# A convolution block on one core: later weights spread over 27 images, small statistics steps on other engines, a new order of the beginning

## The chip, the cores and the metric

The kernel runs on one core of a Trainium2 chip. The metric is the device time of one execution in microseconds; lower is better. The five engines work through queues of their own: TensorE (PE; its weight loads are PEld), VectorE (DVE), ScalarE (ACT), GpSimd (POOL) and SyncE (SP, which here only issues DMAs). They wait for each other by semaphores. A difference of 0.2%, about 2.5 us, is what a measurement of this kernel can tell from no change.

## The reference

`x` holds 160 images of 128 channels, 32 x 32 in float32. Each image is normalised in groups of four channels, the weights are rounded to two coarse levels that depend on the range of all weights, a 3 x 3 convolution runs with one of five weight sets, and the image itself is added.

```python
beta, alpha = max(U), min(U)                  # over all five sets
s1 = (beta - alpha) / 3;   v1 = s1 * floor(U / s1)
s2 = s1 / 5;               v2 = s2 * floor((U - v1) / s2)
w  = (v1 + v2).reshape(128 * 5, 128, 3, 3)
g  = x in 32 groups of 4 channels             # per image
gn = (g - mean(g)) / sqrt(var(g) + 1e-5)
out = x + conv3x3(gn, w, groups=5)            # image 5 b + n uses set n
```

## The kernel before

**Layout.** Channels lie on the 128 partitions, an image is a row of 1024 float32 numbers in each. The images are ordered by weight set: 32 images of set 0, then 32 of set 1 and so on; loads and stores move four images at a time (`load`, `residual`).

**Weights.** `weight_range` (L352) reduces each of the five raw sets to a maximum and a negated minimum on VectorE; `over_partitions` (L365) takes the maximum over the partitions with two TensorE transposes, a VectorE reduction and a TensorE matmul against `ones`, and `Steps.from_range` (L43) derives the step sizes in 20 VectorE instructions on one number per partition. `make_column` (L384) makes one of the three columns of 3 x 3 kernels: 17 VectorE instructions on 128 x 384 numbers (`quantise`, L95, `floor_div`, L81; the last one, L392, writes `m`), then three TensorE transposes (L398), two ScalarE copies (L400, L401) and three GpSimd sums (L403 to L405). It is a generator: `take(column, k)` issues its next k instructions, so that they can be laid between other work. `qpool` has one buffer of each kind.

**Images.** `measure` (L409) finds mean and variance of an image: even ones by VectorE's `bn_stats` (L152, L153), odd ones by two ScalarE passes, sum (L159) and squares (L168), each followed by a small GpSimd step (L161, L162, L171). `Statistics` then goes over a group of up to eight images: `means` (matmul with the group matrix, L177), `deviations` (four VectorE steps, L185 to L189), `variances` (matmul, L192), `scales` (a VectorE step L197, then on GpSimd the power L199 and three small steps L201, L204, L205). `normalise` (L431) and `high_part` (L439) run on ScalarE, `low_part` (L444) and `combinations` (L458 to L461: `d` and `st`) on VectorE. The image is split in a high and a low half-precision part; `conv` (L497) multiplies `st` into the bank pair `m` first (L505), then the high part into `eo` (L478) with `d` (L505). `leave` (L531) copies `m` to `mm` on ScalarE, `add_pairs` makes the pair sums `pq` on VectorE (L540, L541) and TensorE adds them to `eo` (L544). `residual` (L551) adds the image on VectorE and the store is issued on SP. Images 0 to 2 (`FIRST`) go another way: `conv_direct` (L489) adds the high and the low part, 12 matmuls per column of the weights.

**Order.** The order of all instructions is written out by hand in `run` (L562). First come loads and constants, then the beginning up to the three weight columns of set 0, then a loop over the images. In turn i of the loop come: the group matmuls of statistics that are ready, the convolution of image i, the normalisation of i + 3, sums, `leave(i)`, the high part of i + 3, the low part and the combinations of i + 2, `add_pairs(i)`, `residual(i - 1)`, the small statistics steps, the measuring of image i + 13, and the next steps of the next weight set:

```python
if b == self.per_set * 3 // 8 and n + 1 < N_SETS:
    later = (s for col in self.COLS for s in self.make_column(n + 1, col))
if later is not None:
    take(later, 4)
```

`b` counts the images of a set, 0 to 31, so a set's columns are made from image 12 on, four VectorE instructions per image. Each engine works in the order of issue.

The lines that the change touches: `from_range` (L43), `deviations` (L181), `scales` (L194), `weight_range` and `over_partitions` (L352, L365), `measure` (L409), `residual` (L546) and `run` (L562). The functions:

## Time and profile before

| | us |
|---|---|
| median of 3 executions | 1235.76 |
| lowest, highest | 1235.52, 1237.92 |
| profiled execution | 1238.82 |
| its span | 1237.1 |
| TensorE busy | 1134.9 (92%) |
| VectorE busy | 979.9 (79%) |
| ScalarE busy | 678.1 (55%) |
| GpSimd busy | 234.7 (19%) |

The page splits the span in 40 slices of 31 us. TensorE's busy share is below 90% in the slices 1 to 4 and in some later ones, and its granted clock is below full speed in slices 2 to 4. Busy shares are averages over stages with different limits, so what follows goes by stage: which wait ends last there. In rows, `L398` is the line of the kernel; `out<-in` are the program's names; `[1.07 <-DVE m L392]` is the idle time of the engine just ahead of the instruction and what ended it. VectorE instructions of one row overlap a little, so that the distance from start to start is what one costs.

### The profile page before, as it was taken

The numbers are of one execution on the slowest core, as the hardware profiler recorded it, in microseconds if no ns is written. First come the engines' busy times: TensorE is split into PE (matmuls) and PEld (weight loads), VectorE is DVE, ScalarE is ACT, GpSimd is POOL, SyncE is SP. The second block draws the span as 40 slices with busy tenths as digits, with TensorE's granted clock in tenths as the row PEclk, the third lists the DMA queues.
The fourth block names the chain that finished last, engine by engine and source line by source line (L and its number), as shares of the span: only waits on it lengthen the run. The fifth ranks groups of instructions, "written<-read, shape, count | busy, mean of one in ns | idle before, by whom it ended". The sixth has DMA issues, their size and how long they took to land.

```text
span 1237.1 us, 16052 instructions
## 1 busy us (share of the span) xinstructions
PE 1134.9 (92%) x6215; PEld 612.2 (49%) x6215; DVE 979.9 (79%) x1751; ACT 678.1 (55%) x829; POOL 234.7 (19%) x392
## 2 busy tenths in 40 slices
PE   0378999899999998999999999999999999999997
PEld 0134555445555544555555445555544555555553
DVE  7657889987777999777789997777999877777662
ACT  1444755556665555565655555656555565656440
POOL 2121211212121112212121212121112212121100
PEclk9878999999999999999999999999999999999999
DMA  9103333333334333444433333333333444431113
GB/s 379 56 1 134 139 137 136 136 136 137 136 136 152 132 139 129 163 173 179 162 136 136 136 137 136 136 137 138 135 136 137 176 170 179 156 136 69 69 69 138
DMA packets 43140, 171.82 MB, mean 139 GB/s; under 512 B 1456, under 2 KB 1456, under 8 KB 43056
## 3 DMA queue, kind: packets, MB, share of 16 engines
q1 hardware_dynamic: 42768, 169.55, 36.5%
q8 instruction: 50, 0.82, 0.3%
q10 hardware_dynamic: 288, 1.18, 0.2%
q14 instruction: 34, 0.28, 0.1%
HBM read 86.84 MB, written 83.89 MB: 138 GB/s over the span
## 4 chain that ended last, share of the span: by engine, by line
PE 62%; DVE 31%; POOL 3%; issue 2%; ACT 1%; DMA 0%; DVEq 0%; POOLq 0%
PE eo L478 34%; PE m L505 12%; PE eo L505 11%; DVE xt L551 5%; DVE lo L444 4%; PE eo L544 4%; DVE st L152 3%; DVE d L458 2%; DVE pq L541 1%; POOL rstd L199 1%; DVE tt L91 1%; DVE pq L540 1%; DVE tt L92 1%; DVE st L460 1%; DVE tt L89 1%
## 5 line engine op out<-in xcount | busy, mean ns | idle before, releaser
L478 PE MATMUL eo<-hi,wt 128*128 128x512 f16 (+1 forms) x2862 | 690.9, 378 | 1.1 <-ACT wt L400 1.1
L478 PEld LDWEIGHTS <-wt 128*128 128x128 f16 x2934 | 290.2, 99 | 283.6 <-issue 17.2
L505 PEld LDWEIGHTS <-wt 128*128 128x128 f16 x2826 | 277.7, 99 | 221.5 <-issue 8.9
L531 ACT ACTIVATE mm<-m 128x1024 f16<-128x1024 f32 x157 | 160.3, 1021 | 353.3 <-PE m L505 353.1
L505 PE MATMUL eo<-d,wt 128*128 128x256 f16 (+1 forms) x1884 | 283.3, 273 | 0.0
L431 ACT ACTIVATE z<-xt,shift,rstd 128x1024 f32<-128x1024 f32 x160 | 198.1, 1238 | 99.9 <-POOL shift L205 99.9
L505 PE MATMUL m<-st,wt 128*128 128x512 f16 x942 | 235.2, 387 | 3.2 <-DVE xt L551 3.2
L551 DVE SCALAR_TENSOR_TENSOR xt<-eo,s2z,xt 128x1024 f32<-128x1024 f32 x159 | 202.9, 1276 | 8.4 <-PE eo L478 5.9
L444 DVE TENSOR_TENSOR lo<-z,hi 128x1024 f16<-128x1024 f32 x160 | 193.2, 1207 | 3.8 <-ACT hi L439 3.8
L540 DVE TENSOR_TENSOR pq<-mm 128x512 f16<-128x512 f16 x157 | 66.3, 422 | 144.3 <-ACT mm L531 139.4
L439 ACT CAST hi<-z 128x1024 f16<-128x1024 f32 x160 | 165.9, 1037 | 0.2
L458 DVE TENSOR_TENSOR d<-lo 128x1024 f16<-128x1024 f16 x157 | 109.5, 697 | 58.8 <-PE eo L505 48.2
L161 POOL TENSOR_SCALAR minus<-total 128x1 f32<-128x1 f32 x80 | 19.2, 240 | 462.0 <-ACT junk L159 462.0
L152 DVE BATCH_NORM_STATS2 st<-xt 128x6 f32<-128x512 f32 x160 | 102.0, 679 | 0.0
L544 PE MATMUL eo<-pq,up 128*128 128x512 f16 x314 | 93.5, 379 | 7.6 <-DVE pq L541 7.6
L171 POOL TENSOR_SCALAR mv<-squares 128x1 f32<-128x1 f32 x80 | 52.7, 660 | 231.4 <-ACT junk L168 231.4
L168 ACT ACTIVATE junk<-xt,minus 128x1024 f16<-128x1024 f32 x80 | 91.9, 1149 | 1.8 <-POOL minus L161 1.8
L159 ACT ACTIVATE junk<-xt 128x1024 f16<-128x1024 f32 x80 | 83.5, 1044 | 9.7 <-DMA xt<-in_x_dram 9.7
L199 POOL TENSOR_TENSOR rstd<-ve,mhalf 128x8 f32<-128x8 f32 (+2 forms) x23 | 47.2, 2052 | 167.3 <-DVE ve L197 167.3
L460 DVE TENSOR_TENSOR st<-lo 128x512 f16<-128x512 f16 x157 | 67.5, 430 | 0.0
L461 DVE TENSOR_TENSOR st<-lo 128x512 f16<-128x512 f16 x157 | 66.5, 423 | 0.0
L541 DVE TENSOR_TENSOR pq<-mm 128x512 f16<-128x512 f16 x157 | 65.5, 417 | 0.0
(89 smaller groups left out, 450.9 us busy)
## 6 DMA issues: line engine op xcount, KB each, us to landing
xt<-in_x_dram SPq DMA_DIRECT2D x39, 2048.0 KB, 12.6
out_dram<-xt SPq DMA_DIRECT2D x39, 2048.0 KB, 7.6
xt<-in_x_dram SPq DMA_DIRECT2D x4, 512.0 KB, 9.7
out_dram<-xt SPq DMA_DIRECT2D x4, 512.0 KB, 3.7
u<-in_L_conv_U_dram SPq DMA_DIRECT2D x3, 576.0 KB, 7.6
u<-in_L_conv_U_dram ACTq DMA_DIRECT2D x2, 576.0 KB, 6.6
```

The lines of the kernel that those rows point to most:

```text
L152: self.nc.vector.bn_stats(st[:, h, :], image[:, h * half : (h + 1) * half])
L159: nc.scalar.activation(junk, image, ACTF.Copy, accum_out=total)
L168: nc.scalar.activation(junk, image, ACTF.Square, bias=self.minus[j], accum_out=squares)
L431: nc.scalar.activation(z, self.image(i), ACTF.Identity, bias=st.shift[:, j : j + 1], scale=st.rstd[:, j : j + 1],)
L439: self.nc.scalar.copy(hi.rearrange("p h w -> p (h w)"), self.z[i])
L444: self.nc.vector.tensor_sub(lo[:, 1 : self.H + 1, :].rearrange("p h w -> p (h w)"), self.z.pop(i), self.hi[i].rearrange("p h w -> p (h w)"),)
L458: nc.vector.tensor_sub(d, lo[:, 0:H, :], lo[:, 2 : H + 2, :])
L478: nc.tensor.matmul(target[:, h, r0 - h0 : r1 - h0, c0:c1], self.wts[n, col][:, k, :], tile[:, s0 : s0 + r1 - r0, c0 + dw : c1 + dw], start ...
L505: nc.tensor.matmul(target[:, :, c0:c1], self.wts[n, col][:, kind, :], source[:, :, c0 + dw : c1 + dw], start=start, stop=stop,)
L531: self.nc.scalar.mul(m, self.m.pop(i).rearrange("p a i w -> p a (i w)"), DOWN)
L544: nc.tensor.matmul(to, self.up, pq[:, h], start=False, stop=True)
L551: self.nc.vector.scalar_tensor_tensor(xj, eo.rearrange("p h r w -> p (h r w)"), self.steps.s2z, xj, ALU.mult, ALU.add,)
```

## The change

- **Later weights.** The columns of the next set begin at image 4 of a set, not 12, and two instructions are taken per image, not four: 27 images.
- **Statistics.** `deviations` copies the negated mean with ScalarE (`ngm`) and does its three steps on GpSimd; in `scales` ScalarE copies the variance out of PSUM and one GpSimd step adds EPS and brings the factor in, so that two GpSimd steps behind the power fall away. No VectorE step is left in either.
- **Beginning.** All raw weight sets are loaded on the SP queue, set 0 in two halves, which are also reduced one by one. `from_range` becomes a generator and reads the spread from PSUM; its steps are issued alternately with those of the first column. Images below 8 (`EARLY`) are all measured by ScalarE, pairwise. The order of measuring, statistics, columns and first convolutions is new.
- **Loop.** `residual(i - 1)` is issued ahead of `add_pairs(i)`. The pool of `d` and `st` has four buffers, not three.
- **End.** The last image's residual and store go in two halves.

```diff
     def from_range(self, extg):
...
-        span = col("span")
-        nc.vector.tensor_add(span, extg[:, 0:1], extg[:, 1:2])
-        self.s1 = divide_exact("s1", span, 3.0)
-        self.parts1 = parts("s1", self.s1)
...
+        yield nc.vector.tensor_reduce(span, extg, AX.X, ALU.add)
+        yield from divide_exact("s1", self.s1, span, 3.0)
+        yield from parts(self.parts1, self.s1)
+        yield from divide_exact("s2", self.s2, self.s1, 5.0)
+        yield from parts(self.parts2, self.s2)
...
     def deviations(self):
-        nc.vector.tensor_copy(self.gm, self.pg[:, 0, :])
+        nc.scalar.mul(self.ngm, self.pg[:, 0, :], -1.0)
-        nc.vector.tensor_sub(self.dv, mv[:, :, 0], self.gm)
-        nc.vector.tensor_mul(self.dv, self.dv, self.dv)
-        nc.vector.tensor_add(self.dv, self.dv, mv[:, :, 1])
+        nc.gpsimd.tensor_tensor(self.dv, mv[:, :, 0], self.ngm, ALU.add)
+        nc.gpsimd.tensor_tensor(self.dv, self.dv, self.dv, ALU.mult)
+        nc.gpsimd.tensor_tensor(self.dv, self.dv, mv[:, :, 1], ALU.add)
...
     def scales(self):
-        nc.vector.tensor_scalar_add(ve, self.pg[:, 1, :], EPS)
+        nc.scalar.copy(ve, self.pg[:, 1, :])
+        nc.gpsimd.tensor_scalar(ve, ve, EPS, self.scale**-2, ALU.add, ALU.mult)
         nc.gpsimd.tensor_tensor(self.rstd, ve, self.mhalf[:, : self.nb], ALU.pow)
-        if self.scale != 1.0:
-            nc.gpsimd.tensor_scalar_mul(self.rstd, self.rstd, self.scale)
-        nc.gpsimd.tensor_tensor(self.shift, self.gm, self.rstd, ALU.mult)
-        nc.gpsimd.tensor_scalar_mul(self.shift, self.shift, -1.0)
+        nc.gpsimd.tensor_tensor(self.shift, self.ngm, self.rstd, ALU.mult)
...
-        self.rows = pool("rows", 3)
+        self.rows = pool("rows", 4)
...
     def weight_range(self, us):
+        pieces = [us[0][:, : P // 2], us[0][:, P // 2 :], *us[1:]]
...
     def over_partitions(self, ext1, ident):
...
-        extg = self.const.tile([P, 2], F32, tag="extg", name="extg")
-        nc.vector.tensor_copy(extg, spread)
-        self.steps.from_range(extg)
+        return spread
...
     def measure(self, i, stages=(0, 1)):
-        if i % 2 == 0:
+        if i % 2 == 0 and i >= self.EARLY:
...
     def residual(self, i):
+        halves = [slice(0, 512), slice(512, 1024)] if i == self.imgs - 1 else [slice(0, 1024)]
+        for h in halves:
...
     def run(self):
-            (nc.sync, nc.scalar)[n % 2].dma_start(un, self.uv[n])
+            half = P // 2 if n == 0 else P
+            for c in range(0, P, half):
+                nc.sync.dma_start(un[:, c : c + half], self.uv[n][:, c : c + half])
...
+        spread = self.over_partitions(self.weight_range(self.us), ident)
+        chain = self.steps.from_range(spread)
+        column = self.make_column(0, 1)
+        take(chain, 6)
+        take(column, 1)
+        take(chain, 1)
+        take(column, 1)
+        take(chain, 2)
+        take(column, 1)
+        for _ in range(7):
+            take(chain, 1)
+            take(column, 1)
+        run(chain)
+        measure(0, 1)
+        self.stats[0].means()
         self.stats[0].deviations()
         self.stats[0].variances()
+        measure(2, 3)
         self.stats[0].scales()
+        self.stats[1].means()
         self.normalise(0)
         self.high_part(0)
+        self.stats[1].deviations()
+        self.stats[1].variances()
         self.normalise(1)
         self.high_part(1)
+        self.stats[1].scales()
+        run(column)
         self.low_part(0)
         self.low_part(1)
         self.normalise(2)
         self.high_part(2)
         self.normalise(3)
         self.high_part(3)
+        self.conv_direct(0, 1)
+        self.conv_direct(1, 1)
+        column = self.make_column(0, 0)
+        take(column, 5)
         self.low_part(2)
+        measure(4, 5)
         run(column)
+        measure(6, 7)
         self.conv_direct(2, 1)
+        self.conv_direct(0, 0)
         self.stats[2].means()
         self.stats[2].deviations()
+        self.conv_direct(1, 0)
         self.stats[2].variances()
         self.stats[2].scales()
+        self.conv_direct(2, 0)
+        run(self.make_column(0, 2))
...
-            if i >= self.FIRST:
-                self.add_pairs(i)
             if i < self.FIRST:
                 self.residual(i)
             elif i > self.FIRST:
                 self.residual(i - 1)
+            if i >= self.FIRST:
+                self.add_pairs(i)
...
-            if b == self.per_set * 3 // 8 and n + 1 < N_SETS:
+            if b == self.per_set // 8 and n + 1 < N_SETS:
                 later = (s for col in self.COLS for s in self.make_column(n + 1, col))
             if later is not None:
-                take(later, 4)
+                take(later, 2)
```

## Rows read from the trace of the kernel before

**Rows 1.** the chain that ended last, behind the beginning: start, us, what

```profile
167.45 1.85 POOL rstd L199
...
262.87 2.14 PE m L505 x6
...
400.06 1.85 POOL rstd L199
...
1201.41 1.30 PE m L505 x6
...
1208.26 1.30 PE m L505 x6
```

**Rows 2.** windows: us, busy PE, PEld, DVE, ACT, POOL (instructions), PEclk, DMA, GB/s

```profile
264.00:266.00 2.00, 2.00 (x6) 0.71 (x5) 1.64 (x3) 1.65 (x3) 1.32 (x2) 0.50 1.03 406
...
300.00:396.00 96.00, 96.00 (x539) 52.82 (x538) 72.87 (x129) 58.55 (x70) 18.26 (x26) 1.00 0.38 140
```

**Rows 3.** what TensorE waited for from 130 us on: us, times, longest

```profile
PE pt L398 <- DVE m L392: 20.3, 12, 2.3
PE eo L544 <- DVE pq L541: 7.6, 14, 0.9
PE pg L192 <- DVE dv L189: 3.2, 4, 0.8
```

**Rows 4.** the timeline, from the third column's seventh step to its last

```profile
74.16 0.55 DVE L93 TENSOR_TENSOR k<-nn,tt 128x384 f32<-128x384 f32 x1
...
79.89 0.56 DVE L392 SCALAR_TENSOR_TENSOR m<-k,k 128x384 f16<-128x384 f32 x1
```

**Rows 5.** the timeline in the third set, where a weight column ends

```profile
664.37 0.35 PE L398 MATMUL pt<-ident,m 128*128 128x128 f16 x3 [1.07 <-DVE m L392]
```

**Rows 6.** the chain that ended last, up to image 3

```profile
39.72 7.70 PE eo L478 x24
...
65.58 5.07 PE eo L478 x24
...
81.57 4.74 PE eo L478 x12
...
86.34 1.28 DVE xt L551
...
97.90 2.72 PE m L505 x6
```

**Rows 7.** the timeline of VectorE and ScalarE in the beginning

```profile
6.00 1.35 DVE L357 TENSOR_REDUCE ext<-u 128x1 f32<-128x1152 f32 x1 [5.08 <-DMA u<-in_L_conv_U_dram]
...
12.88 1.06 ACT L159 ACTIVATE junk<-xt 128x1024 f16<-128x1024 f32 x1 [9.67 <-DMA xt<-in_x_dram]
...
18.73 0.16 DVE L362 TENSOR_REDUCE ext<-ext 128x2 f32<-128x10 f32 x1
...
21.68 0.16 DVE L68 TENSOR_TENSOR span<-extg 128x1 f32<-128x1 f32 x1
...
24.96 0.47 DVE L87 TENSOR_SCALAR nn<-u,s1r 128x384 f32<-128x384 f32 x1
...
38.03 0.56 DVE L392 SCALAR_TENSOR_TENSOR m<-k,k 128x384 f16<-128x384 f32 x1
```

**Rows 8.** groups by line, operation, shape: busy us, mean ns of one | idle before

```profile
L168 ACT ACTIVATE junk<-xt,minus 128x1024 f16<-128x1024 f32 x80 | 91.9, 1149 | 1.8 <-POOL minus L161 1.8
...
L152 DVE BATCH_NORM_STATS2 st<-xt 128x6 f32<-128x512 f32 x160 | 102.0, 679 | 0.0
...
L204 POOL TENSOR_TENSOR shift<-gm,rstd 128x8 f32<-128x8 f32 x18 | 8.7, 482 | 1.5
```

**Rows 9.** the timeline, the pair sums of the image that starts at 1201.41

```profile
1203.80 0.42 DVE L540 TENSOR_TENSOR pq<-mm 128x512 f16<-128x512 f16 x1 [1.42 <-ACT mm L531]
```

**Rows 10.** the timeline, a small GpSimd step beside VectorE

```profile
402.10 1.22 DVE L444 TENSOR_TENSOR lo<-z,hi 128x1024 f16<-128x1024 f32 x1
...
402.37 1.00 POOL L204 TENSOR_TENSOR shift<-gm,rstd 128x8 f32<-128x8 f32 x1
```

More of the change, by code (lines that the diff above doesn't have):

```diff
@@ L36, in __init__ @@
         self.pool = pool
-        self.s2z = self.col("s2z")
+        self.s1, self.s2, self.s2z = (self.col(tag) for tag in ("s1", "s2", "s2z"))
+        self.parts1, self.parts2 = (
+            tuple(self.col(tag + part) for part in ("r", "nr", "hi", "lo"))
+            for tag in ("s1", "s2")
+        )
         self.far = self.col("fari", I32)
@@ L62, in parts @@
+        def parts(out, s):
+            r, nr, hi, lo = out
+            yield nc.vector.reciprocal(r, s)
+            yield nc.vector.tensor_single_scalar(
                 hi.bitcast(I32), s.bitcast(I32), -4096, op=ALU.bitwise_and
             )
-            nc.vector.tensor_sub(lo, s, hi)
-            return r, nr, hi, lo
+            yield nc.vector.tensor_sub(lo, s, hi)
+            yield nc.vector.tensor_scalar_mul(nr, r, -1.0)
         span = col("span")
-        nc.vector.tensor_add(span, extg[:, 0:1], extg[:, 1:2])
@@ L254, in general_path @@
                     xt.rearrange("p (h w) -> p h w", w=W),
-                    stats.gm, stats.rstd, ALU.subtract, ALU.mult,
+                    stats.ngm, stats.rstd, ALU.add, ALU.mult,
                 )
@@ L291 @@
     LOAD_LEAD = 17
+    EARLY = 8
     FIRST = 3
@@ L354, in weight_range @@
         nc, P = self.nc, self.P
-        ext = self.const.tile([P, 2, N_SETS], F32, tag="ext", name="ext")
-        for n in range(N_SETS):
-            nc.vector.tensor_reduce(ext[:, 0, n : n + 1], us[n], AX.XY, ALU.max)
+        pieces = [us[0][:, : P // 2], us[0][:, P // 2 :], *us[1:]]
+        ext = self.const.tile([P, 2, len(pieces)], F32, tag="ext", name="ext")
+        for k, piece in enumerate(pieces):
+            nc.vector.tensor_reduce(ext[:, 0, k : k + 1], piece, AX.XY, ALU.max)
             nc.vector.tensor_reduce(
-                ext[:, 1, n : n + 1], us[n], AX.XY, ALU.min, negate=True
+                ext[:, 1, k : k + 1], piece, AX.XY, ALU.min, negate=True
             )
@@ L371, in over_partitions @@
             nc.tensor.transpose(rows[:, k, :], ext1[:, k : k + 1], ident)
-        yield
         top = self.const.tile([1, 2], F32, tag="top", name="top")
         nc.vector.tensor_reduce(top, rows, AX.X, ALU.max)
-        ones = self.const.tile([1, P], F32, tag="ones", name="ones")
-        nc.vector.memset(ones, 1.0)
         spread = self.ps_tr.tile([P, 2], F32, tag="pt", name="spread")
-        nc.tensor.matmul(spread, ones, top, start=True, stop=True)
-        yield
-        extg = self.const.tile([P, 2], F32, tag="extg", name="extg")
-        nc.vector.tensor_copy(extg, spread)
-        self.steps.from_range(extg)
+        nc.tensor.matmul(spread, self.ones, top, start=True, stop=True)
+        return spread
     def make_column(self, n, col):
@@ L590, in run @@
             self.los.append(lo)
-        ext1 = self.weight_range(self.us)
-        over = self.over_partitions(ext1, ident)
-        next(over)
-        self.measure(1)
-        self.measure(0)
-        next(over)
-        self.stats[0].means()
-        run(over)
-        column = self.make_column(0, 1)
+        self.ones = self.const.tile([1, P], F32, tag="ones", name="ones")
+        nc.vector.memset(self.ones, 1.0)
+        spread = self.over_partitions(self.weight_range(self.us), ident)
         def take(steps, count):
@@ L633, in run @@
         self.high_part(3)
-        take(column, 6)
+        self.conv_direct(0, 1)
+        self.conv_direct(1, 1)
+        column = self.make_column(0, 0)
+        take(column, 5)
         self.low_part(2)
+        measure(4, 5)
         run(column)
+        measure(6, 7)
         self.conv_direct(2, 1)
-        for i in range(self.FIRST):
-            self.conv_direct(i, 0)
-        column = self.make_column(0, 2)
-        for i in range(4, 8):
-            self.measure(i)
+        self.conv_direct(0, 0)
         self.stats[2].means()
-        take(column, 6)
         self.stats[2].deviations()
+        self.conv_direct(1, 0)
         self.stats[2].variances()
-        take(column, 6)
         self.stats[2].scales()
-        run(column)
-        ready, middle, measured, loaded, later = [], [], 8, 3, None
+        self.conv_direct(2, 0)
+        run(self.make_column(0, 2))
+        ready, middle, measured, loaded, later = [], [], self.EARLY, 3, None
         for i in range(self.imgs):
```

63 lines of the change are left out of this document (22 added, 41 removed).

## The prediction

> **What bounds the kernel now.** I read the 40 slices of the page first, then TensorE's waits, then the timeline where it waits. The slices show a beginning of about 100 us in which TensorE is often idle and its clock granted in part, and a long full stretch behind it. There TensorE sets the time: 6.85 us from image to image [rows 1]; from 300 to 396 us it is busy for all 96.00, VectorE for 72.87 [rows 2]. That is 14 images, so VectorE has 5.2 us of work for each. TensorE's waits behind 130 us are short: 20.3 us in 12 waits for a weight column (`m`), 7.6 for the pair sums `pq`, 3.2 for the deviations `dv`, 31.1 in all [rows 3]. All lie where VectorE also makes the next set's weights. A column is 17 steps; from the seventh to the last are 5.73 us [rows 4], 0.57 a step. Four steps an image make 5.2 + 2.3 = 7.5 us against 6.85: over 13 images VectorE falls some 8 us behind, and TensorE, which transposes each column in its own order, stands until `m` comes [rows 5]. 31.1 / 4 stages = 7.8 agrees. Behind such a wait the granted clock is 0.50, that is 1.2 GHz, for a while [rows 2]: six matmuls that take 1.30 us in a late image take 2.14 [rows 1].
>
> **The beginning.** Images 0 to 2 are convolved column by column, and image 3 starts at 97.90 [rows 6]. I lay the new order out engine by engine with the durations of before.
>
> *Range of the weights.* Ten reductions run from 6.00 to 18.73, 1.27 each [rows 7]; the first waits 5.2 us for a 576 KB slice that shares the transfer engines with the next one. The new first piece is half as large and alone in front. No row shows a half piece: it gains nothing at worst, and 2.6 if its 5.2 us halve. I take 1.5, since the start of a transfer doesn't halve. The other slices come behind it in one queue while VectorE, at 2.5 us a slice, works on the first. The range ends at 17.2.
>
> *Range to first column step.* From 18.73 to 21.68 come transposes, spread and, in between, an image's statistics and `ones`; from 21.68 to 24.96 twenty small steps, each behind the one before, 0.16 us each [rows 7]. Statistics and `ones` leave the first part (1.36 for the two halves [rows 8], of which TensorE's own transposes hid some: 0.9), the copy of the spread too; six steps of the second remain in front. 2.0 + 1.1 = 3.1 (at most 2.95 + 1.1): first column step at 20.4 instead of 24.96. The other 15 small steps go between column steps, where I cost each at 0.1, between nothing and 0.16.
>
> *First column.* 17 x 0.57 + 15 x 0.1 = 11.2: it ends at 31.6, not 38.59, because deviations and a low part no longer stand between its steps [rows 7]. The first convolution is 1.1 us behind (39.72 [rows 6] - 38.59): 32.7, 7 us earlier.
>
> *What ScalarE must have ready.* It now measures images 0 to 3 alone, two passes each of 1.15 us at most [rows 8]. Image data are there from 12.88 [rows 7], so images 0 and 1 are done before 18. Their mean stands behind the spread on TensorE, 19.7; the negated copy, three GpSimd steps and the variance end near 22; but four passes of images 2 and 3 are queued on ScalarE ahead of the variance's copy: 20 + 4.6 = 24.6. With some 2 us for `rstd` and `shift`, z and hi (1.2 and 1.0 us) of image 0 are ready at 29.3, of image 1, with `ngm` of the next group between, at 31.8. VectorE asks for them at 31.6 and 32.8: it just holds, with 1 to 2 us in hand.
>
> *Second and third column.* VectorE: two low parts of 1.2 to 34.0, five steps and a low part to 38.0, twelve steps to 44.8, the third column without a break to 54.5 (before, the statistics of images 4 to 7 stood in it; they are now ScalarE's, done at 51). TensorE: images 0 and 1 take 7.7 us [rows 6] from 32.7; it waits until 45.4; then 12 matmuls of image 2 at the lower clock, 4.74, and 36 more, of which 24 take 5.07 [rows 6], and two group matmuls: 45.4 + 4.7 + 7.6 + 0.7 = 58.4. Now TensorE, not VectorE, is the later one. Transposes and copy: 59.5. Image 0's last 12 matmuls take 2.5 at the full clock, or 4.74 at 1.2 GHz, the other bound [rows 6]: its residual starts at 62.0 instead of 86.34. The row of residuals, low parts and combinations from there to image 3 stays, 97.90 - 86.34 = 11.6 us [rows 6]: image 3 starts at 73.6, **24.3 us earlier**. Bounds: 17 (ScalarE late by 3, the lower clock, nothing from the half piece) to 28 (chain steps and half piece at their best).
>
> **The weights over 27 images.** Two steps an image: 5.2 + 1.1 = 6.3 us, under 6.85, so VectorE no longer falls behind. Within an image: `pq` starts 2.4 us behind the image's first matmul [rows 1, 9] and takes 0.8; statistics of an even image 1.4 [rows 8] and two steps 1.1 end at 5.7, and the transposes are due at 6.85: 1.1 us in hand where `m` came 1.07 late before [rows 5]. So the 31.1 us of waits go, and with them at least one stretch at the lower clock a stage: 2 x 0.84 = 1.7 each (two runs of six matmuls [rows 1]), 6.8 in four. 37.9. A check from outside: from one stage's `rstd` to the next are 400.06 - 167.45 = 232.6 us [rows 1] for 32 images, 219.2 at 6.85 and some 2.2 of group matmuls and transposes: 11.2 lost a stage, 44.8 in all, 7 more than I can name. What stays: the copies of a column on ScalarE wait for the transposes and push the next `mm` and `pq` back by about 2 us, near the end of the image; I leave 3.5 us for that in all, and count half of the unnamed 7. **38 us**, bounds 22 and 44.
>
> **What takes over the moved work.** ScalarE gets two small copies out of PSUM per group of eight images. No row shows so small a copy; it costs more than nothing and less than a pass over an image, 1.15 [rows 8]; nearer to nothing, for 8 columns instead of 1024: 0.2. ScalarE is busy for 58.55 of 96 us [rows 2], and both stand behind `hi`, where no part of the image in work waits for it. GpSimd gets three small steps for `dv` and one for `ve`, and loses two. TensorE asks for `dv` at the next image's start. The copy ends about 3.8 us into the image, a small GpSimd step is 0.48 in the mean [rows 8] and 1.00 at the longest seen here [rows 10]: 5.2 to 6.8, due at 6.85. I take 0. VectorE loses five small steps per group, 0.1 us an image. A fourth row buffer takes away waits of VectorE alone. The residual ahead of `add_pairs` fills VectorE's wait for `mm`. Both cost nothing while VectorE has its 0.5 us an image; without that cover, 1.28 us of residual [rows 6] stand ahead of each `pq`.
>
> That step of 1.00 us ended with the VectorE `lo` beside it [rows 10]. The Trainium skill, "SBUF — State Buffer", Who interferes with whom, calls it an exclusive lock: a VectorE instruction with two SBUF inputs and a GpSimd instruction that reads SBUF exclude each other for their whole length. By it each of the three `dv` steps can be held behind a VectorE instruction, which is rival 3.
>
> **The end.** The last residual, 1.28 us [rows 6], goes in halves: the first store starts 0.64 earlier, the second is half as large. 0.7, between 0 and 1.3.
>
> **Sum.** 24.3 + 38 + 0.7 = 63.0. The profiled execution took 1238.82 (span 1237.1), 3.06 above the median of 1235.76. It becomes 1175.8, and the median **1172.8**.
>
> **Rivals.**
> 1. The columns still hold TensorE: some 20 of the 38 us stay, 1193. For it: only 1.1 us in hand. Against: VectorE is no longer behind on the average. 0.15.
> 2. ScalarE becomes the bound of the beginning: sixteen passes, 18 us, in one order with z, hi and the weight copies. If it is 5 us late twice, image 3 starts at 83.6: 1183. Against: the 1 to 2 us in hand. 0.13.
> 3. GpSimd holds TensorE: each `dv` step waits for a VectorE instruction of 1.2 us like the one in [rows 10]; 3.8 + 3 x 1.2 = 7.4, 0.5 late, and as much again through `shift` and z: 20 groups x 1 us, 1193. 0.07.
> 4. Slower: VectorE becomes the bound of the whole run, as 108 images now carry weight steps. It decides from 6.85 us of VectorE's work an image, where I count 6.3; every 0.1 above costs 10.8 us, 63 are eaten up at 7.4, and at 7.55 the time is 1248. GpSimd and ScalarE with their new steps would have to hold VectorE for over 1.1 us an image. 0.02.
> 5. The interleaving doesn't do what it says (chain steps still cost 0.16 each, the half piece lands no earlier): 2.5 us back, 1175, inside the forecast's width.
>
> **Chances.** The forecast (1164 to 1182, with rival 5) 0.63. The range, 1163 to 1193, takes in rival 2 and most of 1 and 3. A measurement here tells 0.2%, 2.5 us, from nothing: faster 0.96, within 0.01, slower 0.03.
>
> **What would show it.** Image 3's first matmul near 73.6; the first `m` near 31.6; TensorE's waits behind 130 us under 5 us, none for `m` above 0.5; granted clock 1.00 through the stages; 222 us from one stage to the next. Wrong, if TensorE waits for GpSimd's `dv`, if z of image 0 starts later than 29, or if `pq` is what TensorE waits for in every image.

## The result and the profile after

The changed kernel takes 1166.72 us (median of 4, 1165.83 to 1167.89); the kernel before, run beside it, 1236.84. The ratio is 0.9433, 95% interval 0.9417 to 0.945: faster by 5.7%, 6 us below the forecast of 1172.8 and inside its range.

First the changed kernel's page: TensorE's busy share and its granted clock, in tenths, in the span's 40 slices of 29 us.

```profile
PE   0679999999999999999999999999999999999997
...
PEclk9889999999999999999999999999999999999999
```

TensorE is full from the fourth slice to the last but one. The view of what TensorE waited for has no line at all behind 130 us, where [rows 3] had three. From image 3 to TensorE's last matmul it looks like this, in the window view (us, busy time and instructions of PE, PEld, DVE, ACT, POOL, then granted clock, DMA share, GB/s), first after, then before:

```profile
73.60:1158.50 1084.90, 1084.88 (x6080) 595.21 (x6079) 902.51 (x1516) 649.66 (x824) 207.41 (x378) 1.00 0.39 145
```

```profile
97.90:1228.80 1130.90, 1099.91 (x6080) 596.17 (x6079) 912.62 (x1616) 646.62 (x784) 212.02 (x338) 0.99 0.37 139
```

The profiled execution of the kernel before (1238.82) lies 2.0 us above the median beside it, that of the changed kernel (1166.93) 0.2, so the spans differ by 71.9 us (1237.1 to 1165.2) where the medians differ by 70.1; every distance below that starts from the profile of before may be up to 2 us too large by it. The 71.9 came from three places:

| where | before | after | gain | forecast |
|---|---|---|---|---|
| up to image 3's first matmul | 97.90 | 73.62 | 24.3 | 24.3 |
| image 3 to the last matmul | 1130.9 | 1084.9 | 46.0 | 38 (22 to 44) |
| last matmul to the end | 8.3 | 6.7 | 1.6 | 0.7 (0 to 1.3) |

The same 6080 matmuls in the middle line lost 31.0 us of idle time (1130.90 - 1099.91) and also 15.0 us of busy time (1099.91 - 1084.88).

The beginning, in the timeline of the changed kernel (start, us, engine, line, operation; in brackets the idle time before it and what ended it), where [rows 7] stood before:

```profile
3.74 0.75 DVE L361 TENSOR_REDUCE ext<-u 128x1 f32<-128x576 f32 x1 [2.66 <-DMA u<-in_L_conv_U_dram]
...
8.36 1.35 DVE L361 TENSOR_REDUCE ext<-u 128x1 f32<-128x1152 f32 x1 [1.89 <-DMA u<-in_L_conv_U_dram]
...
18.56 0.17 DVE L366 TENSOR_REDUCE ext<-ext 128x2 f32<-128x12 f32 x1
...
21.74 0.48 DVE L90 TENSOR_SCALAR nn<-u,s1r 128x384 f32<-128x384 f32 x1
...
31.53 0.56 DVE L389 SCALAR_TENSOR_TENSOR m<-k,k 128x384 f16<-128x384 f32 x1
...
33.70 2.60 PE L475 MATMUL eo<-hi,wt 128*128 128x512 f16 x6 [0.57 <-ACT wt L397]
...
45.82 0.50 PE L395 MATMUL pt<-ident,m 128*128 128x128 f16 x3 [5.72 <-DVE m L389]
...
61.98 1.28 DVE L550 SCALAR_TENSOR_TENSOR xt<-eo,s2z,xt 128x1024 f32<-128x1024 f32 x1 [6.08 <-PE eo L475]
...
73.62 2.72 PE L502 MATMUL m<-st,wt 128*128 128x512 f16 x6 [3.18 <-DVE xt L550]
```

The reader sees the first column end at 32.1 (31.53 + 0.56), TensorE start its convolutions 1.6 us behind it, and image 3 start 24.3 us earlier than the last line of [rows 6].

### The profile page after: what moved, and what is told of

The parts are those of the page before. It is cut to its first block, busy times and chain, and to the rows that moved or that the text cites. A ratio compares the mean times of both kernels' runs of the same rounds, so it can differ in the third digit from the quotient of the medians.

```text
span 1165.2 us, 15925 instructions
## 1 busy us (share of the span) xinstructions
PE 1116.1 (96%) x6215; PEld 610.4 (52%) x6215; DVE 962.5 (83%) x1626; ACT 690.4 (59%) x891; POOL 234.5 (20%) x450
## 4 chain that ended last, share of the span: by engine, by line
PE 95%; DVE 3%; ACT 1%; DMA 1%; POOL 0%; issue 0%; SPq 0%; DVEq 0%
PE eo L475 52%; PE eo L502 18%; PE m L502 18%; PE eo L541 6%; PE m L475 1%; DMA u<-in_L_conv_U_dram 1%; DVE ext L361 0%; DVE ext L362 0%; DVE xt L550 0%; DVE lo L441 0%; PE pg L196 0%; PE pg L181 0%; POOL rstd L204 0%; PE pt L395 0%; ACT z L428 0%
## 5 line engine op out<-in xcount | busy, mean ns | idle before, releaser
L550 DVE SCALAR_TENSOR_TENSOR xt<-eo,s2z,xt 128x1024 f32<-128x1024 f32 (+1 forms) x160 | 203.5, 1273 | 47.9 <-PE eo L541 40.1
L502 PE MATMUL m<-st,wt 128*128 128x512 f16 x942 | 230.4, 381 | 3.2 <-DVE xt L550 3.2
L428 ACT ACTIVATE z<-xt,shift,rstd 128x1024 f32<-128x1024 f32 x160 | 198.0, 1237 | 31.1 <-POOL shift L207 31.1
L165 POOL TENSOR_SCALAR minus<-total 128x1 f32<-128x1 f32 x84 | 47.3, 563 | 340.9 <-ACT junk L163 340.7
L172 ACT ACTIVATE junk<-xt,minus 128x1024 f16<-128x1024 f32 x84 | 96.7, 1152 | 1.0 <-POOL minus L165 1.0
L156 DVE BATCH_NORM_STATS2 st<-xt 128x6 f32<-128x512 f32 x152 | 97.2, 681 | 0.0
L163 ACT ACTIVATE junk<-xt 128x1024 f16<-128x1024 f32 x84 | 88.0, 1048 | 11.8 <-DMA xt<-in_x_dram 11.7
L175 POOL TENSOR_SCALAR mv<-squares 128x1 f32<-128x1 f32 x84 | 45.7, 545 | 237.5 <-ACT junk L172 234.9
L204 POOL TENSOR_TENSOR rstd<-ve,mhalf 128x8 f32<-128x8 f32 (+2 forms) x23 | 43.9, 1907 | 1.9
```

Of the source, the lines that this page charges most:

```text
L156: self.nc.vector.bn_stats(st[:, h, :], image[:, h * half : (h + 1) * half])
L163: nc.scalar.activation(junk, image, ACTF.Copy, accum_out=total)
L172: nc.scalar.activation(junk, image, ACTF.Square, bias=self.minus[j], accum_out=squares)
L428: nc.scalar.activation(z, self.image(i), ACTF.Identity, bias=st.shift[:, j : j + 1], scale=st.rstd[:, j : j + 1],)
L502: nc.tensor.matmul(target[:, :, c0:c1], self.wts[n, col][:, kind, :], source[:, :, c0 + dw : c1 + dw], start=start, stop=stop,)
L550: self.nc.vector.scalar_tensor_tensor(xj[:, h], eo.rearrange("p h r w -> p (h r w)")[:, h], self.steps.s2z, xj[:, h], ALU.mult, ALU.add,)
```

## The experiments

The question of the middle line was which of the loop's edits earned it: the spreading of the weights, the order of residual and pair sums, the statistics on other engines, or the fourth row buffer. I held theory A, the forecast's: VectorE's rate alone, so that spreading earns nearly all of it. Its rival B: the order of work inside an image, so that the other edits earn much of it too. Four kernels told them apart, each edit shown against the kernel that it starts from.

**Spreading alone**, on the kernel before:

```diff
-            if b == self.per_set * 3 // 8 and n + 1 < N_SETS:
+            if b == self.per_set // 8 and n + 1 < N_SETS:
...
-                take(later, 4)
+                take(later, 2)
```

> The kernel before with one edit: later weights from image 4 of a set, two steps an image. Theory A (VectorE's rate): the stages lose time only because VectorE has 7.5 us of work an image against TensorE's 6.85; at two steps it has 6.3, so nearly all of the stages' 46.0 us goes although order, row buffers and statistics are as before: 40 to 46 us off, 1191 to 1197, TensorE's waits behind 130 us under 5 us. Theory B (order within an image): m, pq and dv come late because of where they stand in VectorE's order and what they wait for, so the new order, the fourth buffer and the moved statistics are needed: under 25 us off, above 1211, waits for m of about 1 us in each of 12 columns.

Measured: 1197.39, ratio 0.9676 (0.966 to 0.9692). From image 3 to the end of the span it is 39.6 us shorter than before (1099.6 against 1139.2). What TensorE still waits for behind 130 us (us in all, times, longest):

```profile
PE pt L398 <- DVE m L392: 4.4, 4, 1.1
...
```

**Spreading undone**, on the changed kernel:

```diff
-            if b == self.per_set // 8 and n + 1 < N_SETS:
+            if b == self.per_set * 3 // 8 and n + 1 < N_SETS:
...
-                take(later, 2)
+                take(later, 4)
```

> The changed kernel with the spreading alone undone: four steps an image from image 12. Theory A: VectorE is over 6.85 us again (7.4 without the small statistics steps), so 30 to 45 us come back: 1197 to 1212, waits for m again the largest of TensorE's behind 100 us. Theory B: order, buffers and statistics cover most of it: under 15 us come back, below 1182.

Measured: 1183.25, ratio 0.9559 (0.9543 to 0.9575), only 16.5 us above the changed kernel. Image 3 starts where it did (73.66). Behind 130 us TensorE waits for:

```profile
PE eo L541 <- DVE pq L538: 6.2, 12, 0.6
PE pt L395 <- DVE m L389: 6.2, 8, 1.1
```

**The other loop edits undone**, on the changed kernel, spread kept:

```diff
-        self.ngm = self.tile("ngm", [self.nb])
-        nc.scalar.mul(self.ngm, self.pg[:, 0, :], -1.0)
+        self.gm = self.tile("gm", [self.nb])
+        nc.vector.tensor_copy(self.gm, self.pg[:, 0, :])
...
-        nc.scalar.copy(ve, self.pg[:, 1, :])
...
+        nc.vector.tensor_scalar_add(ve, self.pg[:, 1, :], EPS)
...
-        self.rows = pool("rows", 4)
+        self.rows = pool("rows", 3)
...
+            if i >= self.FIRST:
+                self.add_pairs(i)
             if i < self.FIRST:
                 self.residual(i)
```

> The changed kernel with three parts undone at once: statistics' small steps on VectorE again, residual behind add_pairs again, three row buffers again. Theory A: they are worth nothing in the loop at 6.3 us of VectorE work an image; what they cost is in the beginning alone, where the statistics' steps stand between column steps: 1166 to 1171, no TensorE wait behind 130 us above 1 us in total. Theory B: 15 us or more come back, above 1181, with waits for pq or m.

Measured: 1186.19, ratio 0.9585 (0.9569 to 0.9601), 19.5 us above the changed kernel. Only 7.3 of it lie behind image 3; 11.8 lie ahead of it (image 3 at 85.39), where I had looked for a cost, but allowed some 4 at most (1171 against 1166.7).

**The same edits alone**, the other way round, on the kernel before:

> The kernel before with the same three parts alone: statistics' small steps on ScalarE and GpSimd, residual ahead of add_pairs, four row buffers. Theory A: VectorE goes from 7.5 to 7.4 us an image in the 13 images, the fourth buffer lets it start up to one image ahead: at most 15 us off, 1221 to 1237, m still late. Theory B: 25 us or more off, below 1211.

Measured: 1194.4, ratio 0.9654 (0.9638 to 0.967). Image 3 starts at 82.97, 14.9 earlier than before, and from there to the end it is 29.6 shorter. Behind 130 us TensorE has the same two waits as with the spreading undone, 6.2 and 6.2 us.

Theory A falls as the sole cause. It fits spreading alone, but it allowed the other edits 15 us at most and they bring 42.8 (14.9 of it ahead of image 3), and by it undoing the spreading would have cost 30 to 45, where it cost 16.5. Theory B as it stood falls too: it allowed spreading alone less than 25 us, and that brought 39.8. The two groups stand in for each other: of the 47.6 us behind image 3 (1139.2 to 1091.6) either spreading alone (39.6) or the other edits alone (29.6) take most, and each adds much less on top of the other: 7.3 and 16.9. Why they overlap by so much was not followed through the traces.

**Which of the other edits**: theory C holds that it is the order, D the statistics, E the row buffers. Each alone, on the kernel before:

```diff
-            if i >= self.FIRST:
-                self.add_pairs(i)
             if i < self.FIRST:
                 self.residual(i)
             elif i > self.FIRST:
                 self.residual(i - 1)
+            if i >= self.FIRST:
+                self.add_pairs(i)
```

> The kernel before with one edit: residual of the previous image ahead of add_pairs. Together with the row buffers and the statistics it took 29.6 us off the loop (from image 3's start to the end 1139.2 to 1109.6) and 14.9 off the beginning. Theory C (order): behind pq stood residual, statistics and four steps before m was written, 2.4 + 0.8 + 1.2 + 1.4 + 2.3 = 8.1 us into an image of 6.85, so m is late in every column even without a backlog; without the residual there it is 6.9. Then this edit alone takes 15 to 25 us off the loop, nothing off the beginning: 1212 to 1222, waits for m down from 1.7 us each to about 1. Theory D (statistics): the chain that ended last ran through rstd in every stage, so VectorE's late ve and dv steps set the loss: this edit alone gives under 8 us, above 1229.

Measured: 1220.35, ratio 0.9863 (0.9846 to 0.9879); 18.6 us behind image 3, nothing ahead of it. TensorE's waits:

```profile
PE eo L544 <- DVE pq L541: 14.2, 15, 1.3
PE pt L398 <- DVE m L392: 6.4, 8, 1.1
```

Against [rows 3] the wait for `m` fell from 20.3 to 6.4 and the one for `pq` rose from 7.6 to 14.2, with a longest of 1.3, about the residual of 1.28 us which now stands ahead of `pq`: the edit changes nothing else, but only 15 of the pair sums wait.

The statistics alone (the edits of `deviations` and `scales`, as the change has them):

```diff
...
-        nc.vector.tensor_sub(self.dv, mv[:, :, 0], self.gm)
-        nc.vector.tensor_mul(self.dv, self.dv, self.dv)
-        nc.vector.tensor_add(self.dv, self.dv, mv[:, :, 1])
+        nc.gpsimd.tensor_tensor(self.dv, mv[:, :, 0], self.ngm, ALU.add)
+        nc.gpsimd.tensor_tensor(self.dv, self.dv, self.dv, ALU.mult)
+        nc.gpsimd.tensor_tensor(self.dv, self.dv, mv[:, :, 1], ALU.add)
...
-        nc.vector.tensor_scalar_add(ve, self.pg[:, 1, :], EPS)
+        nc.scalar.copy(ve, self.pg[:, 1, :])
+        nc.gpsimd.tensor_scalar(ve, ve, EPS, self.scale**-2, ALU.add, ALU.mult)
...
```

> The kernel before with one edit: the statistics' small steps on ScalarE and GpSimd. Theory C: off the beginning about 15 us (image 3 at 83 instead of 97.9, as when all three parts were in), under 10 off the loop: 1214 to 1224. Theory D: 15 off the beginning and 20 or more off the loop: below 1203.

Measured: 1204.91, ratio 0.974 (0.9724 to 0.9756): 20.5 us behind image 3, and 13.8 ahead of it (image 3 at 84.12).

```profile
PE pt L396 <- DVE m L390: 15.3, 12, 2.3
PE eo L542 <- DVE pq L539: 3.0, 6, 0.6
```

The wait for `dv` is gone, the one for `m` lost a quarter, and its longest is what it was.

The fourth row buffer alone:

```diff
-        self.rows = pool("rows", 3)
+        self.rows = pool("rows", 4)
```

> The kernel before with one edit: four row buffers. Theories C and D: VectorE's 45 us of waits for a row buffer go, but it waits the same time for mm behind them, so nothing: 1235 to 1239. Theory E (lead): with a fourth buffer VectorE enters each weight stage one image ahead, and up to 6 us per stage of the 11 are covered: 1213 to 1225.

Measured: 1235.29, ratio 0.9981 (0.9971 to 0.999): 1.75 us or 0.2% by the medians, at the edge of what can be told from nothing. What VectorE waited for behind 130 us, before and then with four buffers:

```profile
DVE pq L540 <- ACT mm L531: 134.2, 100, 4.9
DVE d L458 <- PE eo L505: 45.2, 50, 1.0
```

```profile
DVE pq L540 <- ACT mm L531: 181.4, 99, 4.9
```

The fourth buffer took away VectorE's 45.2 us of waiting for a free buffer of `d`, and it waits 47.2 us longer for `mm` instead, as an engine does that isn't the bound. So C and D each hold for their own edit, and E is next to nothing (4 us behind image 3 by the profiles, of which the profile of before may be 2). 18.6, 20.5 and 4.0 make 43.1 where all three together brought 29.6; even with 2 us off each, 37 against 28. These, too, stand in for each other in part.

**The beginning** was forecast to the tenth, so its steps were tried one by one on the changed kernel. The chain run whole ahead of the column, as before, instead of interleaved:

```diff
-        take(chain, 6)
-        take(column, 1)
...
-        for _ in range(7):
-            take(chain, 1)
-            take(column, 1)
         run(chain)
+        take(column, 10)
```

> The changed kernel with the range's whole chain of small steps issued ahead of the first column, nothing interleaved. By the prediction's step (15 steps at 0.16 us each behind the other, instead of 0.1 between column steps): the first column's m 1 us later, image 3's start at 74.5, 1168. If each small step between column steps was free and costs its whole 0.19 us: 3 us later, 76.5. If ScalarE and not VectorE sets the beginning (hi of image 0 ended at 30.2, of image 1 at 32.5): m later, image 3's start the same 73.6.

Measured: 1166.31 (one run), image 3 at 73.07. In that execution the weights' range came 1.3 us earlier by itself (first chain step at 19.29 against 20.58), so the clean figure is the distance from there: to the end of the first column 12.95 instead of 11.51 us, to TensorE's transposes of the second 26.57 (45.86) instead of 25.24 (45.82), to image 3 53.78 instead of 53.04. Interleaving saves 1.4 us on VectorE, of which 1.3 reach the second column. The profile with the spreading undone, whose beginning is that of the changed kernel, has the same 25.24 (20.15 to 45.39). That only 0.7 arrive at image 3 is TensorE's clock: image 2's first twelve matmuls begin at 1.2 GHz in both, and it rose earlier in the serial execution (granted clock from 45 to 52 us 0.76, against 0.66). First the changed kernel, then the serial one:

```profile
46.12 2.71 PE L475 MATMUL m<-hi,wt 128*128 128x512 f16 x6
48.62 1.98 PE L475 MATMUL m<-lo,wt 128*128 128x512 f16 x6
```

```profile
46.16 2.62 PE L475 MATMUL m<-hi,wt 128*128 128x512 f16 x6
48.61 1.43 PE L475 MATMUL m<-lo,wt 128*128 128x512 f16 x6
```

The weights' slices in two DMA queues instead of one:

```diff
-                nc.sync.dma_start(un[:, c : c + half], self.uv[n][:, c : c + half])
+                (nc.sync, nc.scalar)[n % 2].dma_start(un[:, c : c + half], self.uv[n][:, c : c + half])
```

> The changed kernel with the raw weights of sets 1 and 3 issued by ScalarE again; set 0 stays in two halves in front on SP. In the changed kernel the first half came at 3.74, but VectorE then stood 1.9 us for the second slice (8.36), and the range ended at 18.56 against 18.73 before. If the single queue makes the second slice late: slice 1 is there by 6.4, the range ends between 16.3 and 17.0 and image 3 starts near 71.7. If all slices share the transfer engines anyway: the range ends at 17.5 to 18.7 as in the other runs, image 3 at 72.8 to 73.8.

Measured: 1167.32 (one run). The first half is there at 5.20 instead of 3.74, and the range ends at 18.54 instead of 18.56. That is no gain, but it is one execution, and the range's end moves by 1.3 us from one to another (below).

Images 0, 2, 4 and 6 measured by VectorE again:

```diff
-        if i % 2 == 0 and i >= self.EARLY:
-            st.image(j, image)
+        if i % 2 == 0:
+            if 0 in stages or i >= self.EARLY:
+                st.image(j, image)
             return
```

> The changed kernel, but images 0, 2, 4 and 6 measured by VectorE's bn_stats as before. VectorE gets four times 1.4 us, two of them (0 and 2) while the first column is made; ScalarE loses eight passes of 1.1. Theory F (VectorE bounds the beginning up to 58 us): image 3 starts 2.8 to 5.6 us later, 76.4 to 79.2, 1169 to 1173. Theory G (ScalarE bounds it: hi of image 0 came at 30.2 and of image 1 at 32.5, just as VectorE asked for them): image 3 starts at 72 to 74, 1164 to 1167.

Measured: 1175.84 (one run), image 3 at 82.47, 8.9 us later. Between 20 and 130 us TensorE waits longest for:

```profile
PE pg L181 <- DVE mv L157: 12.1, 2, 9.1
...
```

The first group's mean stands behind `mv` in VectorE's order, and z of image 0 starts at 35.48 instead of 27.92 behind it. So measuring the early images on ScalarE is worth some 9 us of the 24.3 with the rest in place and at this place in VectorE's order, behind the first column's steps (with it ahead of them, as before, was not run), and the statistics' small steps some 12 to 14 (the two runs above); the two may overlap, since neither was taken away together with the other.

**A version that beats both.** Ahead of image 3, VectorE is the late engine from 61.98 on. This version takes the statistics of images 8 and 10 from it (ScalarE measures them in its gaps) and puts image 2's residual, for which image 3 waits, ahead of image 4's low part:

```diff
+    ON_ACT = (8, 10)
...
-        if i % 2 == 0 and i >= self.EARLY:
+        if i % 2 == 0 and i >= self.EARLY and i not in self.ON_ACT:
...
         measure(6, 7)
+        measure(8)
...
         self.stats[2].scales()
+        measure(10)
...
+            if i == self.FIRST - 1:
+                self.residual(i)
...
-            if i < self.FIRST:
+            if i < self.FIRST - 1:
...
```

> The changed kernel with the wait before image 3 shortened: images 8 and 10 are measured by ScalarE in gaps it has between 51 and 58 us, and image 2's residual, which frees the bank pair that image 3 needs, is issued ahead of image 4's low part. In the changed kernel TensorE ends image 2 at 67.0, VectorE has two bn_stats (2.9) and a low part with combinations (2.5) ahead of that residual, and image 3 starts at 73.6 at the lower clock (12 matmuls lose 2.4). If VectorE's order is all: image 3 starts at 69.4, the clock stays: 1160 to 1162. If ScalarE's passes push the copies of the third column or z of image 4: 72 or later, 1164 to 1167.

Measured: 1161.16 (1159.95 to 1161.32), ratio 0.9381 (0.9366 to 0.9397), 5.6 us below the changed kernel. Image 3 starts at 69.60, and the clock is whole there; windows around image 3's start, after and then this version:

```profile
66.00:73.60 7.60, 1.45 (x7) 0.67 (x6) 7.53 (x13) 3.75 (x6) 0.91 (x3) 0.78 0.00 0
73.60:78.00 4.40, 4.38 (x14) 1.69 (x14) 3.03 (x6) 1.62 (x2) 0.00 (x0) 0.61 0.00 0
```

```profile
68.00:69.60 1.60, 0.49 (x5) 0.32 (x3) 1.52 (x3) 1.60 (x4) 0.05 (x1) 1.00 0.00 0
69.60:75.00 5.40, 5.40 (x30) 2.89 (x30) 5.33 (x10) 5.11 (x7) 2.24 (x4) 1.00 0.00 0
```

In the changed kernel TensorE is idle for 6.2 of 7.6 us (7.60 - 1.45) and then has a mean granted clock of 0.61, 1.2 GHz for most of the window; in this version it waits 1.1 us and keeps 2.4 GHz. 4.0 us come from the earlier start and 1.7 from the clock (4.38 x 0.39). The clock is no accident of one execution: the mean granted clock of the whole run is 0.996 to 0.998 in the four executions of this version and 0.993 in all four of the changed kernel.

The residual's place alone, without the two images (on the changed kernel):

```diff
+            if i == self.FIRST - 1:
+                self.residual(i)
             if self.FIRST <= i + 2 < self.imgs:
                 self.low_part(i + 2)
                 self.combinations(i + 2)
-            if i < self.FIRST:
+            if i < self.FIRST - 1:
                 self.residual(i)
```

> One of the two edits of the faster variant alone, on the changed kernel: image 2's residual goes ahead of image 4's low part and combinations in VectorE's order; images 8 and 10 stay on VectorE. In the changed kernel VectorE ends the statistics in front of that low part at 69.81, and image 3 starts at 73.62 when that residual has freed its accumulator. The low part and the combinations are 1.17 + 0.61 + 0.34 + 0.34 = 2.5 us from start to start, so image 3 should start at 71.1. If the clock that TensorE is granted then depends on how long it stood before, it is still half (it stands for some 3.6 us of the 4.2 instead of 6.3 of the 6.7; in the faster variant it stood 1.1 in a row and kept the full clock): the 1.7 us of the slow stretch stay, 1164.2. If the slow stretch goes too: 1162.5. If the faster variant's gain came from taking the two images' statistics off VectorE alone: no change, 1166.7.

Measured: 1165.01 (1164.17 to 1166.54), ratio 0.9415 (0.9399 to 0.943): 1.7 us below the changed kernel by the medians, less than the 2.5 that can be told from nothing, so what follows rests on the profiles (span 1162.7 against 1165.2). Image 3 starts at 71.45, TensorE waits 3.0 and then 0.7 us ahead of it, and the clock still falls, though for a shorter while:

```profile
68.00:72.00 4.00, 0.91 (x4) 0.57 (x5) 3.97 (x6) 2.10 (x3) 0.21 (x1) 0.84 0.00 0
72.00:76.00 4.00, 4.00 (x18) 1.77 (x16) 3.93 (x7) 1.80 (x2) 0.00 (x0) 0.73 0.00 0
```

That is the forecast in which the clock stays low: 2.2 us from the start, little from the clock. In these profiles the order alone is worth 2.5 us of span (1165.2 to 1162.7), and the two images' statistics on top of it 3.2 (to 1159.5; 3.85 by the medians): 1.85 of earlier start, and the clock that no longer falls.

## Why the prediction held, and where it did not

**The beginning: 24.3 forecast, 24.3 measured, in part by misses that cancel.** The half piece came 2.26 us earlier than the whole one (3.74 against 6.00), more than the 1.5 taken. But VectorE then stood 1.89 us for the next slice, so the range ended at 18.56 and not at 17.2: my sentence that the other slices come in time behind it was the step that failed. It failed by a term that varies: in the seven profiles with this beginning and one queue the second slice was there between 7.04 and 8.36, and where it came at 7.04 or 7.06 (two of them) the range did end at 17.24 and 17.26. From the range to the first column step were 3.2 us (forecast 3.1; the chain has 21 small steps, six and fifteen, where I wrote twenty). The column took 10.35 us instead of 11.2; run by itself (the serial kernel) it takes 9.95, so the 15 small steps between cost 0.03 each, not 0.1. z and `hi` of images 0 and 1 were ready at 30.2 and 32.5 (29.3 and 31.8 forecast) and asked for at 32.0 and 33.2: 1.8 and 0.7 us in hand where I had said 1 to 2. From there on the layout is met line for line: TensorE's transposes at 45.8 (45.4), its end of the second column at 58.3 (58.4), the first residual at 61.98 (62.0), the row of VectorE to image 3 11.64 (11.6).

What the step didn't say is where the 24.3 come from. It laid out the sum of all edits and never priced an edit of the statistics alone. The runs do: moving the small steps brings 13.8 us in the order of before, 11.8 in the new one. Rival 2, ScalarE as the bound, did not delay it, but it stood near: in the chain of waits of the changed kernel, from 22 to 37.6 us nearly every piece is ScalarE's or GpSimd's.

```profile
23.36 2.26 ACT junk L172 x4
...
33.36 1.57 POOL rstd L204
...
36.50 1.05 ACT hi L436
...
37.65 1.23 DVE lo L441
```

VectorE's low part of image 2 starts at 37.65, within 0.1 us of the work ahead of it and of `hi`: the two engines arrive together, so that a faster VectorE alone would have gained nothing there.

**The weights over 27 images: 38 forecast, 46.0 measured, above the upper bound of 44.** (If the 1.8 us by which the spans differ more than the medians lie here, which no run shows, it is about 44, at the bound.) The 31.1 us of waits went, all of them. The term that was mis-sized is "half of the unnamed 7, and 3.5 that stay". Nothing stays: in the changed kernel the transposes stand without a wait, with `m` done at 260.2 and the transposes at 261.85.

```profile
259.66 0.51 DVE L389 SCALAR_TENSOR_TENSOR m<-k,k 128x384 f16<-128x384 f32 x1
...
261.85 0.33 PE L395 MATMUL pt<-ident,m 128*128 128x128 f16 x3
```

And the unnamed 7 can be named; it was in TensorE's busy time. Two things are in the 15.0 us. First the clock: of its stretches at 0.50 behind a wait in the kernel before I priced four; there are five behind 130 us, and the one at image 3 is shorter now. Windows of the kernel before:

```profile
263.00:267.00 4.00, 4.00 (x13) 1.49 (x12) 3.44 (x7) 3.65 (x6) 1.75 (x3) 0.57 1.03 368
...
495.00:500.00 5.00, 4.84 (x19) 2.22 (x20) 4.01 (x8) 3.59 (x5) 1.75 (x3) 0.66 1.02 354
...
97.90:103.00 5.10, 5.10 (x14) 1.87 (x14) 3.59 (x9) 2.34 (x3) 0.00 (x0) 0.52 0.00 0
```

Busy time times what the clock lacks of 1.00 gives 1.7 for the first stretch (4.00 x 0.43) and 1.6 for the second (4.84 x 0.34); the five together make 8.1, image 3's 2.4 (5.10 x 0.48) against 1.7 after: 8.8 of the 15.0. Second, as an estimate from one wait, a wait costs more than its idle time, because the last matmul runs out alone where the next would have started into it. The kernel before, without and with a wait:

```profile
241.78 0.60 PE L505 MATMUL eo<-d,wt 128*128 128x248 f16 x4
242.22 1.44 PE L478 MATMUL eo<-hi,wt 128*128 128x496 f16 x6
243.49 0.60 PE L505 MATMUL eo<-d,wt 128*128 128x248 f16 x4
245.03 0.59 PE L544 MATMUL eo<-pq,up 128*128 128x512 f16 x2 [0.93 <-DVE pq L541]
```

Four such matmuls take 0.60, and where nothing waits the next group starts 0.44 behind their start (241.78 to 242.22); at 243.49 the next starts after 1.54, of which 0.93 are listed as idle: 1.54 - 0.93 - 0.44 = 0.17 are extra. 30 waits [rows 3] x 0.17 = 5.1. 31.0 + 8.8 + 5.1 = 44.9 of the 46.0. From one stage to the next there are now 220.85 us (365.67 to 586.52, the ends of the same transposes), 222 forecast. The count of images was one too high: 51 steps at two an image end in the 26th image of a stage, not the 27th, so 104 images carry them and not 108; no term of the 38 hangs on it.

The mechanism as told, VectorE falling behind by four steps an image, fits the spreading alone, but it is not the only handle: at the same four steps an image the changed kernel with the spreading undone waits 12.4 us and not 31.1. That the residual's place, the row buffer and VectorE's five small steps earn 0 is true of the changed kernel only in part: undoing all three costs 7.3 us behind image 3, and on the kernel before the order alone earned 18.6. "Both cost nothing while VectorE has its 0.5 us an image" held: behind 130 us nothing waits for `pq`. Without that cover, with the order alone, TensorE waits for `pq` 15 times and up to 1.3 us, the 1.28 that I had named, but not for each.

**What takes over the moved work.** The copies of ScalarE were taken at 0.2 and the `dv` steps of GpSimd at no more than 0.48 to 1.00. Groups by form of the changed kernel (busy us, mean ns of one):

```profile
L189 ACT ACTIVATE ngm<-pg 128x8 f32<-128x8 f32 x18 | 3.3, 181 | 0.0
L201 ACT COPY ve<-pg 128x8 f32<-128x8 f32 x18 | 3.0, 168 | 0.0
```

```profile
L191 POOL TENSOR_TENSOR dv<-mv,ngm 128x8 f32<-128x8 f32 x18 | 4.5, 253 | 95.5 <-ACT ngm L189 80.6 <-issue 14.9
...
```

Rival 3 (GpSimd holds TensorE) didn't happen, and the timeline tells why: the three steps stand beside VectorE's statistics of an image, and the step that does stand beside a low part is held until it ends.

```profile
244.38 1.28 DVE L156 BATCH_NORM_STATS2 st<-xt 128x6 f32<-128x512 f32 x2
...
247.03 1.22 DVE L441 TENSOR_TENSOR lo<-z,hi 128x1024 f16<-128x1024 f32 x1
```

```profile
244.82 0.20 POOL L191 TENSOR_TENSOR dv<-mv,ngm 128x8 f32<-128x8 f32 x1 [5.20 <-ACT ngm L189]
...
245.38 0.20 POOL L193 TENSOR_TENSOR dv<-dv,mv 128x8 f32<-128x8 f32 x1
...
247.14 1.17 POOL L166 TENSOR_SCALAR mv<-total 128x1 f32<-128x1 f32 x1
```

`dv` is done 4.4 us into the image that began at 241.16, 2.4 us before TensorE asks for it. The Trainium skill, "SBUF — State Buffer", Who interferes with whom, says that a VectorE instruction with two SBUF inputs excludes a GpSimd instruction that reads SBUF and one with a single input does not: for these small steps the trace agrees with both halves, 1.17 us beside `lo` (two inputs) and 0.20 beside the statistics (one). For a longer step it doesn't, and the measurement decides: a power of 1.98 us, which reads `ve` and `mhalf`, and the two-input subtraction for `lo` ran at the same time, and `lo` took its usual 1.22.

```profile
252.11 1.98 POOL L204 TENSOR_TENSOR rstd<-ve,mhalf 128x8 f32<-128x8 f32 x1
...
252.48 1.22 DVE L441 TENSOR_TENSOR lo<-z,hi 128x1024 f16<-128x1024 f32 x1
```

**The end: 1.6 against 0.7, above its bound of 1.3.** The two halves of the residual take 1.41 us, 0.13 more than the whole, and the second store, half as large, ends 5.3 us behind its residual (1159.95 to 1165.2) where the whole one needed 7.0 (1230.1 to 1237.1). I had left the store's own shortening out of the bound. A kernel with the last residual whole wasn't run, so how much of the 1.6 is the split's alone stays open.

Of the other rivals, 1 (columns still hold) and 4 (VectorE as the bound) failed on the same row: in 96 us of a stage VectorE is busy for 84.81, 6.06 for each of 14 images where 6.3 were counted.

```profile
300.00:396.00 96.00, 96.00 (x541) 52.75 (x539) 84.81 (x145) 58.95 (x75) 22.22 (x36) 1.00 0.42 155
```

## What to carry to other kernels

When one engine's lateness is spread over short waits, several edits can each take most of it and together not much more; so price an edit on the kernel without the others and again on the kernel with them, and don't add the two. Steps that stand in a bound engine's order at a start (here statistics between the first weights' steps) cost their whole wait downstream, so move them to an engine with slack even if they take longer there. A wait of an engine that feeds its work in a pipe costs its idle time, the run-out of the last piece and, at times, what the clock then lacks.

## What the runs showed of the hardware

- Waits and TensorE's granted clock: behind waits of 1.17 and 1.11 us (at 60.41 and 69.60 of the fastest version) it stayed at 1.00; behind 3.0 and 0.7 us (the residual's place alone) and behind 3.0 and 3.18 (after) it fell to 0.50, and in the kernel before behind 0.78 and 2.26 (at 259.67 and 262.52). Such a stretch cost 1.2 to 2.4 us.
- The waits alone don't decide it, nor do they together with the transfers. In the kernel before, waits of 0.27 and 1.74 us come in all four stages, with a DMA share of 0.15 or 0.16 in the second one and 1.00 to 1.02 in the 3 us behind it. Behind those that end at 230.47 and 463.11 the clock stayed at 1.00; behind those at 695.74 and 928.13 it fell. The windows behind the second and the third (clock, DMA share and GB/s at the end):

```profile
463.11:466.10 2.99, 2.99 (x18) 1.58 (x19) 2.85 (x6) 0.66 (x2) 2.73 (x4) 1.00 1.01 399
695.74:698.70 2.96, 2.96 (x12) 1.27 (x13) 2.82 (x6) 0.66 (x2) 2.70 (x4) 0.66 1.02 401
```

So the full share (1.02 to 1.03) beside all five stretches at 0.50 behind 130 us of that kernel is not enough by itself to bring one, and the stretch at 97.90, with a share of 0.00, shows that none is needed. What decides between equal waits stays open, and with it the price of a wait: up to 1.7 us more or nothing.
- Small steps of VectorE that each need the one before start 0.19 us apart (20.77, 20.96, 21.16, 21.35 in the changed kernel); slipped between larger steps on other data they cost 0.03 each.
- A transfer of half the size came 2.26 us earlier (3.74 against 6.00). When the slice behind it came varied between 7.04 and 8.36 us in seven profiles of the same beginning, and with it what the earlier start gained at the range's end, 0.2 to 1.5 us (18.56 to 17.24 against 18.73).
- Single profiles of a start are good to 1.3 us at the range's end (17.24 to 18.56) and to 2.0 at image 3: the four kernels whose beginning is that of the kernel before have it at 96.27 to 98.26.
